# Moving zeros, source rows and half loads in the opening of a graph message-passing kernel on one Trainium2 core

## The chip, the core and the metric

The kernel runs on one core of one Trainium2 chip. The metric is the device time of one execution in microseconds (us). A core has five engines with their own instruction lists: PE (matrix products), DVE (vector), ACT (scalar functions), POOL (GpSimd, which also issues the indirect transfers) and SP (which issues nearly all other transfers). Sixteen DMA engines carry the transfers that SP and POOL issue.

## The reference

There are 6,250 nodes of 128 features and 200,000 edges, sorted by `dst`. Every edge has 20 attributes and a weight.

```python
def _L0_gnn_ref(atomic_embedding, pair_indices, f_ij, f_ij_cutoff, W_in, W_f1, b_f1, W_f2, b_f2, W_o1, b_o1, W_o2, b_o2):
    idx_i = pair_indices[0]
    idx_j = pair_indices[1]
    x = atomic_embedding @ W_in
    W_ij = shifted_softplus(f_ij @ W_f1 + b_f1) @ W_f2 + b_f2
    W_ij = W_ij * f_ij_cutoff
    x_ij = x[idx_j] * W_ij
    out = jax.ops.segment_sum(x_ij, idx_i, num_segments=N_ATOMS)
    return shifted_softplus(out @ W_o1 + b_o1) @ W_o2 + b_o2
edge_index = jnp.stack([src, dst])
h = jnp.maximum(_layernorm(x, axis=-1), 0.0)
x = x + _L0_gnn_ref(h, edge_index, edge_attr_20, edge_weight1, ...)
```

The gather goes by `dst`, which is sorted, and the sum by `src`, which is not.

## The kernel before, in words

**Quads and items.** The edges are cut into 391 quads of 512. The main loop at L1326 runs over items; item i holds the stages of several quads side by side. PE computes z of quad i+1 (`s1_pe`), ACT its softplus for quad i, DVE the one-hot rows `oh` of quad i (L379), PE the edge filter W (L561) and the gathered rows xg (L553) of quad i-1, DVE their product m (L576). Two quads are computed ahead of the loop. Steps that are not part of this pipeline hang on hooks: `at(i, point, fn, ...)` runs fn in item i at a named point. The point "L" stands first in an item and takes most loads; "D2" stands near its end. A hook's item thus sets its place in every engine's list, and SP issues strictly in that order. SP may have eight transfers under way: an issue waits for the eighth before it (the waits DMAHW0 to DMAHW7 in the order of instructions). POOL's are counted in the same way.

**Loads.** `load_sc(s)` (L337 to L357) loads what two quads need, a set: three parts of `ft`, the split edge attributes, from `fsd` (L344); two of `rb`, the relative node numbers, from `reld` (L348); and four windows `wn` of the node table `tab` (L355). Sets 0 and 1 are loaded ahead of the loop, set i/2 + 2 at the start of each even item. `fsd` is written by the kernel itself in blocks: `fb_load` (L312) brings a block of attributes, `fb_1` to `fb_4` split it in three, and L334 writes it. The largest value of a block is taken by `fb_max` (L321). `sb_load(k)` (L393) brings 16-bit source numbers, `sb`, for two quads to all partitions; it has four buffers.

**Where a sum goes.** From quad 8 on every second quad goes through a permutation on PE (pm, pt, pq, un). The others are compared with their own sources, either one by one (`eq`, L407; PE adds equal sources and copies them as s, L596) or, from quad 17, in pairs with a list (`eql`, L421; counted by PE as `lcnt`, L431). POOL then scatters their rows with an adding indirect transfer (L638) into one of four accumulators in memory. `acc_of(k)` picks the one for the k-th scatter: `K2_END` is where the turn among two, k % 2, becomes a turn among three, k % 3. A scatter that goes to the same accumulator as one before waits for that one to land.

**Zeros.** Each accumulator begins as zeros, written in ten pieces of 128 x 640 (320 KB, `zero_piece`, L201), and a few more for lists (`zero_list`, L205). POOL issues those of the first accumulator (three early, seven at L980) and of the second (L1011 to L1012), SP those of the third in the items of the list `Z2` and of the fourth in `Z3`. Between the first's zeros and the second's POOL copies one element, `gate` (L1010), out of the `wn` of set 1, and so waits until that has landed.

**The half pieces.** `base_i`, `reld` and the 16-bit sources `src16` are made from the raw numbers: for the first half of the kernel ahead of the loop, for the second half in two pieces. `half_load(k)` (L1043, L1044) brings a piece's `dst` and `src` numbers, two transfers of 196 KB. `half_piece(k)` has DVE compute `base_i`, `rel_f` and `rel_b` (L941 to L947), SP write `rel_b` to `reld` (L948), DVE narrow the sources (L891), SP write them to `src16` (L892), and DVE take the extent (`rel_ext`, L952, L953). `rel_b` lies in the one buffer named "x3" and the narrowed sources in the one buffer named "h". The same buffer "h" takes the output of the relu of the node table's next group (`prep_relu`, L271), which PE multiplies by W_in (L278).

Of the kernel before, what the change touches and what calls it, by code (L numbers as in the profile page):

```python
# [8 lines left out]
BF16 = mybir.dt.bfloat16  # L9
# [66 lines left out]
def tile_gnn(ctx: ExitStack, tc: tile.TileContext, x, fB, cT, srcT, srcr, srci, dstr, win_, wf1, wf2, bias, bo1c, wo1,  # L76
             wo2, consts, ident, cmap, out, n_edges):
    nc = tc.nc
# [9 lines left out]
    spread = big(NSC)  # L88
    NCH = -(-n_edges // P)
    NQ = -(-NCH // 4)  # L90
# [6 lines left out]
    GN = NP // GRP  # L97
    ZR = 10 if ACC_R % 10 == 0 else 1
    ZEARLY = 3
    K1_END, K2_END, K3_END = 0, 16, 170  # L100
    Z2, Z3 = [0, 1, 1, 2, 2, 3, 3, 4, 4, 5], range(18, 58, 4)
    mpq = sorted_quads(NQ)
    mpi = {q: n for n, q in enumerate(mpq)}
    rounds = unit_rounds(mpq)
# [92 lines left out]
    def zero_piece(eng, k, j, parts=1):  # L197
        v = accs[k][:ACC_R].rearrange("(p t) f -> p (t f)", p=P).rearrange("p (r e) -> r p e", r=ZR)
        w = ACC_R // ZR // parts
        for h in range(parts):  # L200
            eng.dma_start(v[j][:, h * w:(h + 1) * w], zero[:, :w])  # L201
# [692 lines left out]
    with tc.manual_schedule():  # L894
# [83 lines left out]
        nc.gpsimd.tensor_copy(b2rep, b2p.unsqueeze(1).to_broadcast([P, 4, P]))  # L978
        for j in range(ZEARLY, ZR):
            zero_piece(nc.gpsimd, 0, j)  # L980
        ms = []
        for i in range(2):
            m_ = cp.tile([P, 4, 132], F32, name=f"m{i}")
# [22 lines left out]
        sb_load(0)  # L1006
        if NQ > 2:
            load_sc(1)
            gate = cp.tile([1, 1], BF16, name="gate")
            nc.gpsimd.tensor_copy(gate, loads[1][2][0:1, 0, 0:1])  # L1010
        for j in range(ZR):  # L1011
            zero_piece(nc.gpsimd, 1, j)  # L1012
        if NB > 1:
            fb_load(1)
        hooks = {}
# [1 line left out]
        def at(i, point, fn, *a):  # L1017
            hooks.setdefault((i, point), []).append((fn, a))
# [8 lines left out]
            for fn, a in hooks.pop((i, point), []):  # L1027
                fn(*a)

        at(2 if spread else 0, "D2", rel_ext, 0, rel0)  # L1030
        if CE < EP // P:
            w = (CE + 4 * NS) // 2
            for i, a, b in ((8, CE, w), (10, w, 4 * NS), (13, CB, EP // P)):
# [17 lines left out]
            rel_ext(1 + k, r)  # L1051

        for k in range(2):
            at(k + 1 if spread else 0, "L", half_load, k)
            at(2 * k + 3 if spread else 0, "D2", half_piece, k)
        for j in range(ZR):
            at(Z2[j] if spread else 0, "L", zero_piece, nc.sync, 2, j)
        for j in range(ZR):
# [20 lines left out]
        for b in range(1, NB):  # L1079
            t0 = 2  # L1080
            if b > 1:
                t0 = 8 * b - 8
                while t0 + 1 not in mpi or t0 + 1 in units:
                    t0 -= 1
                at(max(0, t0 - 6), "L", fb_load, b)
            if b > 1:
                put("fmax", t0, fb_max, b)
            else:
                at(2, "D2", fb_max, b)
            put("f1", t0, fb_1, b)  # L1090
            put("f2", t0, fb_2, b)
            put("f3", t0, fb_3, b)
            put("f4", t0, fb_4, b)
# [118 lines left out]
        for r in range(-(-len(mpq) // RKQ)):  # L1212
# [10 lines left out]
            k = max(k + 1, i + AT["rk_slot"][0])  # L1223
            assert k <= i + 1
            at(k, AT["rk_slot"][1], rank_slot, r)
        for k in range(1, -(-NS // 2)):
            if not LB <= 2 * k < LE:
                at(max(0, splain[2 * k] - 4), "L", sb_load, k)
        for w in range(NW):
# [87 lines left out]
        for q in range(first):  # L1317
            s3_pe(q)
            s3_copy(q, 0)
            s3_copy(q, 1)  # L1320
            s3_idx(q)
            s3_ji(q)
            s3_scatter(q)
        consts_late()
        s1_pe(first)
        for i in range(max(NQ + 7, last + 22, r0_end + 2, lend + 24)):  # L1326
            if i % 2 == 0 and i // 2 + 2 <= (NQ - 1) // 2:
                load_sc(i // 2 + 2)
            run(i, "L")
            run(i, "D0")  # L1330
            if first <= i < NQ:
                s1_oh(i)
            run(i, "D1")
            if first <= i - 1 < NQ:
                s1_eq(i - 1)
            run(i, "PE0")
            if first <= i - 1 < NQ:
                s2_pe_x(i - 1)
            if first <= i and i + 1 < NQ:
                s1_pe(i + 1)  # L1340
            if first <= i - 1 < NQ:
                s2_pe_w(i - 1)
            run(i, "PEZ")
            if first <= i < NQ:
                s1_exp(i)
                run(i, "AE")
                s1_ln(i)
            else:
                run(i, "AE")
            if first <= i - 3 < NQ and not full[i - 1]:  # L1350
                s3_copy(i - 3, 0)
                s3_copy(i - 3, 1)
            run(i, "A0")
            if first <= i - 4 < NQ:
                s3_ji(i - 4)
            run(i, "A1")
            if first <= i - 1 < NQ:
                s2_copy(i - 1)
            run(i, "AX")
            run(i, "DM")  # L1360
            if first <= i - 1 < NQ:
                s2_m(i - 1)
            if first <= i - 3 < NQ:
                s3_idx(i - 3)
            run(i, "DR")
            run(i, "PE1")
            full[i] = sum(fn in banked for fn, _ in hooks.get((i, "PE2"), [])) > 2
            if first <= i - 2 < NQ:
                s3_pe(i - 2)
                if full[i]:  # L1370
                    s3_copy(i - 2, 0)
                    s3_copy(i - 2, 1)
            run(i, "PE2")
            run(i, "A2")
            run(i, "D2")
            if first <= i - 4 < NQ and plainq(i - 4):
                s3_scatter(i - 4)
            if first <= i - 2 < NQ and i - 2 not in mpi and not plainq(i - 2):
                s3_scatter(i - 2)
            run(i, "S")  # L1380
# [365 lines left out]
```

## Time and profile before

| | us |
|---|---|
| three timed runs | 1917.05, 1916.89, 1916.43 |
| their median | 1916.89 |
| the profiled execution's own time | 1913.6 |
| its span, first to last instruction | 1911.6 |

| engine | busy us | share of the span |
|---|---|---|
| PE | 1807.8 | 95% |
| DVE | 1656.5 | 87% |
| POOL | 1517.3 | 79% |
| ACT | 1476.1 | 77% |

The mean granted PE clock is 0.980 of full speed. The profile's times count from the start of the span. A timeline row has the start, the duration, the engine, the line of the code, the operation, what it writes and reads, and a count; in brackets stands the idle time of that engine just before, with what ended it. For SP (SPq) a row is the issue of a transfer, not its flight. Which wait ended last is inferred, so the name in brackets can be that of a semaphore that came last by the profile though another one held.

### The profile page before, as it was taken

The numbers are of one execution on the slowest core, as the hardware profiler recorded it, in microseconds if no ns is written. First come the engines' busy times: TensorE is split into PE (matmuls) and PEld (weight loads), VectorE is DVE, ScalarE is ACT, GpSimd is POOL, SyncE is SP. The second block draws the span as 40 slices with busy tenths as digits, with TensorE's granted clock in tenths as the row PEclk, the third lists the DMA queues.
The fourth block names the chain that finished last, engine by engine and source line by source line (L and its number), as shares of the span: only waits on it lengthen the run. The fifth ranks groups of instructions, "written<-read, shape, count | busy, mean of one in ns | idle before, by whom it ended". The sixth has DMA issues, their size and how long they took to land.

```text
span 1911.6 us, 58074 instructions
## 1 busy us (share of the span) xinstructions
PE 1807.8 (95%) x20601; PEld 1218.7 (64%) x20601; DVE 1656.5 (87%) x4692; ACT 1476.1 (77%) x4045; POOL 1517.3 (79%) x965
## 2 busy tenths in 40 slices
PE   4679999999999999999999999999999999999986
PEld 3556666666666666666666666666666666666654
DVE  5588998889999999999999889889889889888767
ACT  4579878878887878878887787787787787787725
POOL 4677887788886888888888888888888888878755
PEclk8799999999999999999999999999999999999998
DMA  8888787767775777776776677667666676666648
GB/s 286 205 175 167 155 179 140 132 120 131 139 134 114 131 129 128 132 148 119 128 138 127 123 128 129 117 130 127 116 129 129 115 130 126 118 116 134 106 100 268
DMA packets 351703, 267.55 MB, mean 140 GB/s; under 512 B 96719, under 2 KB 315258, under 8 KB 351410
## 3 DMA queue, kind: packets, MB, share of 16 engines
q1 hardware_dynamic: 218516, 197.30, 35.7%
q0 software_dynamic: 132336, 66.32, 34.7%
q8 instruction: 162, 2.65, 0.6%
q14 instruction: 131, 1.07, 0.2%
q10 hardware_dynamic: 558, 0.20, 0.0%
HBM read 154.65 MB, written 109.00 MB: 138 GB/s over the span
## 4 chain that ended last, share of the span: by engine, by line
PE 69%; DVE 16%; DMA 5%; POOL 2%; issue 2%; SPq 2%; ACT 1%; DVEq 0%; POOLq 0%; ACTq 0%
PE pq L743 20%; PE un L839 17%; PE W L561 13%; PE z L362 5%; PE po L756 4%; DVE pm L718 3%; PE xg L553 2%; PE W L550 2%; DMA acc<-s,lji 2%; DVE pt L732 2%; DVE so L824 2%; POOL acc L638 2%; DVE s L576 1%; DMA sb<-src 1%; DVE pt L576 1%
## 5 line engine op out<-in xcount | busy, mean ns | idle before, releaser
L638 POOL DMA_INDIRECT acc<-s,lji x751 | 1208.2, 1609 | 255.4 <-issue 176.2
L743 PE MATMUL pq<-pt,pm 128*128 128x387 bf16 x3056 | 582.9, 337 | 1.2 <-ACT s L596 0.6
L566 ACT ACTIVATE xc<-xg,cb 128x128 f32<-128x128 f32 x1564 | 448.0, 375 | 140.5 <-PE xg L553 130.6
L749 ACT CAST mst<-pq 128x387 bf16<-128x387 f32 x764 | 364.2, 487 | 93.0 <-PE pq L743 87.5
L561 PEld LDWEIGHTS W<-w,a 128*128 128x128 f32 x3128 | 421.6, 195 | 17.9 <-issue 6.9
L743 PEld LDWEIGHTS <-pm 128*128 128x128 bf16 x3056 | 294.3, 98 | 197.5 <-issue 4.5
L561 PE MATMUL W<-w,a 128*128 128x128 f32 x3128 | 419.9, 278 | 0.0
L839 PE MATMUL un<-so,mst 32*128 32x392 bf16 x9168 | 409.0, 325 | 9.4 <-DVE rank L685 4.3
L839 PEld LDWEIGHTS <-mst 32*128 32x128 bf16 x9168 | 240.4, 93 | 152.0 <-issue 16.7
L372 ACT ACTIVATE a<-a,con 128x512 f32<-128x512 f32 x391 | 282.5, 723 | 11.6
L732 DVE TENSOR_TENSOR pt<-pt 128x512 f32<-128x512 f32 x382 | 260.6, 682 | 0.0
L718 DVE TENSOR_SCALAR pm<-iotp,pos 128x576 bf16<-128x576 f16 x764 | 255.9, 395 | 0.0
L367 ACT ACTIVATE a<-z 128x512 f32<-128x512 f32 x391 | 236.4, 605 | 6.1 <-PE z L362 6.1
L850 DVE TENSOR_TENSOR accT<-un,accT 128x392 f32<-128x392 f32 x368 | 182.2, 556 | 47.8 <-PE un L839 47.4
L638 POOL DMA_INDIRECT acc<-os,oji x108 | 182.6, 1690 | 51.2 <-issue 12.2
L824 DVE TENSOR_SCALAR so<-iot,mst 128x392 bf16<-128x392 f16 x764 | 217.6, 335 | 2.1 <-PE un L839 2.0
L576 DVE TENSOR_TENSOR pt<-W,xc 128x512 f32<-128x512 f32 x191 | 131.5, 688 | 67.5 <-PE po L756 33.7
L362 PE MATMUL z<-ft,ws 123*128 123x512 bf16 x391 | 154.1, 395 | 17.2 <-DMA ft<-fsd 10.0
L576 DVE TENSOR_TENSOR s<-W,xc 128x512 f32<-128x512 f32 x188 | 128.5, 684 | 47.8 <-ACT xc L566 41.6
L553 PE MATMUL xg<-wn,oh 63*128 63x128 bf16 x1564 | 156.3, 221 | 13.2 <-DVE oh L379 11.3
L550 PE MATMUL W<-b2rep,onesb 64*128 64x512 bf16 x391 | 152.8, 391 | 0.0
L638 POOL DMA_INDIRECT acc<-s,ji x48 | 79.4, 1655 | 40.4 <-DMA acc<-s,ji 19.2
(216 smaller groups left out, 1794.2 us busy)
## 6 DMA issues: line engine op xcount, KB each, us to landing
rb<-reld SPq DMA_DIRECT2D x391, 64.0 KB
sb<-src SPq DMA_DIRECT2D x192, 128.0 KB
fsd<-f SPq DMA_DIRECT2D x49, 480.0 KB
ft<-fsd SPq DMA_DIRECT2D x195, 120.0 KB
fb<-in_fB_dram SPq DMA_DIRECT2D x49, 320.0 KB
ft<-fsd SPq DMA_DIRECT2D x195, 80.0 KB
wn<-tab SPq DMA_DIRECT2D x782, 15.8 KB
acc<-s,lji POOLq DMA_INDIRECT x751
```

Of the source, the lines that this page charges most:

```text
L362: nc.tensor.matmul(z, ws, ft[:K1, j * SEG:(j + 1) * SEG], start=True, stop=True)
L372: nc.scalar.activation(a, a, AF.Ln, bias=half, scale=0.5)
L561: nc.tensor.matmul(W[:, c, :], st[q]["a"][:, c * P:(c + 1) * P], w2, start=False, stop=(c == 3))
L566: nc.scalar.mul(xc[:, c, :], st[q]["xg"][:, c, :], late["c", q // CQ][:, 4 * (q % CQ) + c:4 * (q % CQ) + c + 1])
L576: nc.vector.tensor_tensor(m[:, :, :P], st[q]["W"], st[q]["xc"], op=ALU.mult)
L638: nc.gpsimd.indirect_dma_start(out=accs[k][:rows, :], out_offset=bass.IndirectOffsetOnAxis(ap=ji, axis=0), in_=s, in_offset=None, compute_ ...
L718: nc.vector.tensor_scalar(pm[:, c], iotp, rk[r]["pos"][:, 4 * j + c:4 * j + c + 1], None, op0=ALU.is_equal)
L732: nc.vector.tensor_tensor(pt[:, :, k * P:(k + 1) * P], a, high(a), op=ALU.subtract)
L743: nc.tensor.matmul(t[:, :PW], mp[q]["pm"][:, c, s * P:(s + 1) * P], high(mp[q]["pt"][:, c:c + 1, :PW])[:, 0], start=(c == 0), stop=(c == 3))
L749: nc.scalar.copy(mp[q]["ms", s][:, :PW], mp[q].pop(("q", s))[:, :PW])
L824: nc.vector.tensor_scalar(so, iotw[:, :GN], w[:, 3 * P // 2:3 * P // 2 + 1], None, op0=ALU.is_equal)
L839: nc.tensor.matmul(ts[g][:, :GN], mp[q]["ms", s][v, k * P:(k + 1) * P], mp[q]["oh"][v], start=(q == qs[0] and k == 0), stop=(q == qs[-1] a ...
```

## The change

The change edits no computation. It edits when steps of the opening are issued:

- `K2_END` goes from 16 to 24: eight more scatters take turns between two accumulators. `Z2` goes from items 0 to 5 to items 2 to 8.
- The second accumulator's ten zeros follow the first's seven on POOL directly; `gate` is gone.
- `sb_load(1)` is issued right behind set 1 and ahead of `fb_load(1)`, and no longer in the loop.
- `half_load(0)` and `(1)` go from items 1 and 2 to 4 and 5, `half_piece(0)` and `(1)` from items 3 and 5 to 6 and 7, `rel_ext(0)` from item 2 to 5, and `fb_max(1)` from item 2 to 3.
- z and `oh` of quad 2 stand ahead of `consts_late`, a row of small DVE steps.

```diff
-    K1_END, K2_END, K3_END = 0, 16, 170
-    Z2, Z3 = [0, 1, 1, 2, 2, 3, 3, 4, 4, 5], range(18, 58, 4)
+    K1_END, K2_END, K3_END = 0, 24, 170
+    Z2, Z3 = [2, 3, 4, 5, 5, 6, 6, 7, 7, 8], range(18, 58, 4)
...
         for j in range(ZEARLY, ZR):
             zero_piece(nc.gpsimd, 0, j)
+        for j in range(ZR):
+            zero_piece(nc.gpsimd, 1, j)
...
             load_sc(1)
-            gate = cp.tile([1, 1], BF16, name="gate")
-            nc.gpsimd.tensor_copy(gate, loads[1][2][0:1, 0, 0:1])
-        for j in range(ZR):
-            zero_piece(nc.gpsimd, 1, j)
+        if spread:
+            sb_load(1)
         if NB > 1:
             fb_load(1)
...
-        at(2 if spread else 0, "D2", rel_ext, 0, rel0)
+        at(5 if spread else 0, "D2", rel_ext, 0, rel0)
...
-            at(k + 1 if spread else 0, "L", half_load, k)
-            at(2 * k + 3 if spread else 0, "D2", half_piece, k)
+            at(k + 4 if spread else 0, "L", half_load, k)
+            at(k + 6 if spread else 0, "D2", half_piece, k)
...
-                at(2, "D2", fb_max, b)
+                at(3 if spread else 1, "D2", fb_max, b)
...
-        for k in range(1, -(-NS // 2)):
+        for k in range(2 if spread else 1, -(-NS // 2)):
...
-        consts_late()
         s1_pe(first)
+        s1_oh(first)
+        consts_late()
...
-            if first <= i < NQ:
+            if first < i < NQ:
                 s1_oh(i)
```

Three places show how the lists of SP and DVE read before and after. The first is SP's list between set 3 and set 4, before; `half` is a half load, `acc` from `zero` a zero piece, `xt` the node table's next group, `reld` and `src` the first half piece's two writes:

```order
L1043 DMA half<-in_dstr_dram 98x512 [waits DMAHW0_49]
L1044 DMA half<-in_srci_dram 98x512 [waits DMAHW1_49]
L201 DMA acc_77<-zero 128x640 [waits DMAHW2_49]
L201 DMA acc_77<-zero 128x640 [waits DMAHW3_49]
L393 DMA sb<-src_81 128x1024 [waits DMAHW4_49]
L201 DMA acc_77<-zero 128x640 [waits DMAHW5_49]
L201 DMA acc_77<-zero 128x640 [waits DMAHW6_49]
L225 DMA xt<-in_x_dram 128x256 [waits DMAHW7_49]
L948 DMA reld<-rel_b 98x512 [waits DMAHW0_49,DVE_49]
L892 DMA src_81<-s_523 98x512 [waits DMAHW1_49,DVE_49]
L334 DMA fsd<-f_468 128x3x640 [waits DMAHW2_49,DVE_49]
L344 DMA ft_120<-fsd 60x1024 [waits DMAHW3_49,DMAHW2_49,PE_49]
```

The same place in the changed kernel:

```order
L201 DMA acc_77<-zero 128x640 [waits DMAHW3_49]
L393 DMA sb<-src_81 128x1024 [waits DMAHW4_49]
L201 DMA acc_77<-zero 128x640 [waits DMAHW5_49]
L225 DMA xt<-in_x_dram 128x256 [waits DMAHW6_49]
L334 DMA fsd<-f_456 128x3x640 [waits DMAHW7_49,DVE_49]
L344 DMA ft_120<-fsd 60x1024 [waits DMAHW7_49,DMAHW0_49,PE_49]
```

Six issues stand less between set 3 and the write of `fsd`; ahead of set 3 a half load and three zeros have gone as well.

The second place is SP's list between set 5 and set 6 of the changed kernel (before, the writes of `reld` and `src` for the second half piece stood ahead of set 5, and those of the first ahead of set 4). It begins with the second of the two zeros behind set 5:

```order
L201 DMA acc_77<-zero 128x640 [waits DMAHW1_49]
L393 DMA sb<-src_81 128x512 [waits DMAHW2_49,DVE_49]
L393 DMA sb<-src_81 128x512 [waits DMAHW3_49]
L205 DMA acc_76<-zero 128x384 [waits DMAHW4_49]
L948 DMA reld<-rel_b 98x512 [waits DMAHW5_49]
L892 DMA src_81<-s_707 98x512 [waits DMAHW6_49]
L201 DMA acc_77<-zero 128x640 [waits DMAHW7_49]
L201 DMA acc_77<-zero 128x640 [waits DMAHW0_49]
L393 DMA sb<-src_81 128x512 [waits DMAHW1_49,DVE_49]
L393 DMA sb<-src_81 128x512 [waits DMAHW2_49]
L205 DMA acc_77<-zero 128x384 [waits DMAHW3_49]
L948 DMA reld<-rel_b 98x512 [waits DMAHW4_49]
```

Both pieces' writes now stand between set 5 and set 6, each behind source rows that wait for DVE, and the second's `src` write follows the last row.

The third place is DVE's list at the second half piece. Before, in item 5:

```order
L576 TENSOR_TENSOR m_255<-W,xc 128x4x128 [waits PE_49,Activation_49]
L612 SCALAR_TENSOR_TENSOR jf<-s,con,jd 128x4
L233 BN_STATS bn<-xt 128x6 [waits DMAHW7_49]
L233 BN_STATS bn<-xt 128x6
L235 BN_AGGR mv<-bn 128x2 [waits DVE_49] x2
L237 TENSOR_SCALAR var<-mv 128x2 [waits DVE_49]
L941 TENSOR_SCALAR base_i<-half,con 98x2 [waits DMAHW0_49]
L943 TENSOR_TENSOR rel_f<-half,base_i 98x512 [waits DVE_49]
L947 TENSOR_SCALAR rel_b<-rel_f 98x512 [waits DMAHW0_49,DVE_49]
L891 CAST s_651<-half 98x512 [waits DMAHW1_49]
```

The changed kernel, in item 7:

```order
L421 TENSOR_TENSOR eql<-sb,srcT_sb 128x1024 [waits DMAHW5_49,DMAHW4_49]
L576 TENSOR_TENSOR m_265<-W,xc 128x4x128 [waits PE_49,Activation_49]
L608 TENSOR_SCALAR jd<-srcT_sb,con 128x16
L612 SCALAR_TENSOR_TENSOR jf<-s,con,jd 128x4 [waits DVE_49]
L941 TENSOR_SCALAR base_i<-half,con 98x2 [waits DMAHW6_49]
L943 TENSOR_TENSOR rel_f<-half,base_i 98x512 [waits DVE_49]
L947 TENSOR_SCALAR rel_b<-rel_f 98x512 [waits DMAHW5_49,DVE_49]
L891 CAST s_795<-half 98x512 [waits DMAHW7_49,DMAHW6_49]
L952 TENSOR_REDUCE ext<-rel_f 98x1
L953 TENSOR_REDUCE ext<-rel_f 98x1
L325 TENSOR_TENSOR fr<-fb,f_766 128x640
```

The piece now stands behind the list's compare, and its `rel_b` and its narrowed sources wait for the transfers that free their one buffer each.

More of the change, by code (lines that the diff above doesn't have):

```diff
@@ L1323, in tile_gnn @@
             s3_scatter(q)
+        s1_pe(first)
+        s1_oh(first)
         consts_late()
-        s1_pe(first)
         for i in range(max(NQ + 7, last + 22, r0_end + 2, lend + 24)):
```

## The prediction, as put on record

> **What bounds the kernel now.** I read the table by stretch first. Its columns are the stretch in us, its length, and for each engine the busy us (with instructions), then the granted clock, the busy share of the DMA engines and GB/s.
>
> ```profile
> 25.00:30.00 5.00, 4.55 (x19) 3.56 (x19) 2.32 (x8) 2.42 (x7) 2.33 (x6) 1.00 0.63 194
> 30.00:35.00 5.00, 2.16 (x11) 1.88 (x12) 4.75 (x20) 3.87 (x9) 3.18 (x6) 0.73 1.03 406
> ...
> 80.00:90.00 10.00, 8.15 (x86) 7.32 (x86) 7.52 (x20) 9.28 (x28) 4.95 (x3) 0.82 0.63 155
> 90.00:100.00 10.00, 7.56 (x51) 5.34 (x50) 4.35 (x11) 7.20 (x20) 7.16 (x5) 0.83 0.87 213
> ...
> 150.00:200.00 50.00, 48.78 (x520) 32.66 (x519) 44.60 (x126) 44.58 (x126) 39.46 (x25) 1.00 0.81 171
> ```
>
> From 150 us on PE works 48.78 of 50 us: nothing moved in the opening can make that part shorter. The change acts in the opening, where PE has gaps, and its worth is how much earlier (or later) the kernel comes into the steady part. Second, I read the timelines of DVE, ACT and PE between 70 and 103 us for the idle times (start, us of work, instruction, and in brackets the idle time ahead and who ended it).
>
> ```profile
> 72.81 0.69 DVE L421 TENSOR_TENSOR eql<-sb,srcT_sb 128x1024 bf16<-128x1024 int16 x1 [4.41 <-DMA sb<-src]
> ...
> 78.00 0.38 ACT L271 ACTIVATE h<-hps 128x256 f32<-128x256 f32 x1 [10.60 <-DMA ft<-fsd]
> ...
> 84.51 0.69 DVE L421 TENSOR_TENSOR eql<-sb,srcT_sb 128x1024 bf16<-128x1024 int16 x1 [1.69 <-DMA sb<-src]
> ...
> 94.40 0.69 DVE L421 TENSOR_TENSOR eql<-sb,srcT_sb 128x1024 bf16<-128x1024 int16 x1 [3.40 <-DMA sb<-src]
> ...
> 97.94 0.82 DVE L321 TENSOR_REDUCE fmax<-fb 128x1 f32<-128x640 f32 x1 [2.25 <-DMA fb<-in_fB_dram]
> ...
> 101.60 0.69 DVE L421 TENSOR_TENSOR eql<-sb,srcT_sb 128x1024 bf16<-128x1024 int16 x1 [0.74 <-DMA sb<-src]
> ...
> 102.35 0.38 PE L431 MATMUL lcnt<-wgtb,eql 128*128 128x1 bf16 x8 [4.79 <-DVE eql L421]
> ```
>
> The waits are for loads that SP issues, so SP's place in its list decides. The relu at 78.00 is a case where the named releaser is not the true one. The relu writes buffer h, whose last content is the 16-bit copy of a half piece; it must wait until that copy's write, issued at 72.87 (row below), has landed: 5.1 us. I measure the change at two marks: that relu, and PE's lcnt at 102.35.
>
> **The change part by part.** SP's list from the third set of loads to the fifth is the first place. Columns as above; x1 to x4 are issues.
>
> ```profile
> 35.38 1.19 SPq L201 DMA_DIRECT2D acc<-zero  x1
> ...
> 39.28 1.07 SPq L1043 DMA_DIRECT2D half<-in_dstr_dram  x1
> 40.40 0.39 SPq L1044 DMA_DIRECT2D half<-in_srci_dram  x1
> 40.83 0.84 SPq L201 DMA_DIRECT2D acc<-zero  x2
> ...
> 52.39 2.40 SPq L201 DMA_DIRECT2D acc<-zero  x2
> 54.83 0.51 SPq L225 DMA_DIRECT2D xt<-in_x_dram  x1
> 55.44 1.56 SPq L948 DMA_DIRECT2D reld<-rel_b  x1
> ...
> 57.58 0.41 SPq L334 DMA_DIRECT2D fsd<-f  x1
> 61.88 1.09 SPq L344 DMA_DIRECT2D ft<-fsd  x3
> ...
> 65.21 1.76 SPq L355 DMA_DIRECT2D wn<-tab  x4
> ...
> 72.87 0.45 SPq L892 DMA_DIRECT2D src<-s  x1
> 74.54 1.11 SPq L344 DMA_DIRECT2D ft<-fsd  x3
> ...
> 78.25 1.76 SPq L355 DMA_DIRECT2D wn<-tab  x4
> 80.11 0.83 SPq L393 DMA_DIRECT2D sb<-src  x2
> ...
> 83.00 2.02 SPq L344 DMA_DIRECT2D ft<-fsd  x3
> ...
> 96.01 1.45 SPq L344 DMA_DIRECT2D ft<-fsd  x3
> ```
>
> *Ahead of the write of fsd (57.58), a gain.* Five of the third accumulator's zeros leave this stretch: 1.19 + 0.84 + 2.40 = 4.4 us. So do both half loads: 1.07 + 0.39 for the first and, at the bare 0.39 an issue, 0.8 for the second: 2.2 us. So do the first half piece's two writes: 1.56 + 0.45 = 2.0 us. Together 8.6 us. With no gate POOL's zeros start to fill the stretch 25 to 30, which ran at a DMA share of 0.63: up to 0.37 x 5 = 1.8 us of transfers come out of the crowd behind. The write of fsd would then go out at 57.6 - 8.6 - 1.8 = 47.2. Source rows for quads 2 and 3, now ahead of the second edge attributes, are on that same list and cost it nothing; they take away DVE's first long wait, below, and the front of DVE runs with this lead.
>
> *The lead is then paid back.* The half loads now stand behind the fourth set. From the write of fsd to its readers took 61.88 - 57.58 = 4.3 us, the set itself to 65.21 + 1.76 = 66.97, so 5.1 us: the first half load goes out at 47.2 + 4.3 + 5.1 = 56.6. DVE now stands at that half piece in item 6 without other work. Its rows of before, and the two waits behind transfers that give a landing:
>
> ```profile
> 43.90 0.76 DVE L407 TENSOR_TENSOR eq<-sb,srcT_sb 128x256 f32<-128x256 int16 x2 [6.05 <-DMA sb<-src]
> ...
> 59.51 0.49 DVE L233 BATCH_NORM_STATS2 bn<-xt 128x6 f32<-128x128 f32 x2 [4.50 <-DMA xt<-in_x_dram]
> ...
> 60.33 0.22 DVE L941 TENSOR_SCALAR base_i<-half,con 98x2 int32<-98x2 int32 x1
> ...
> 61.65 0.42 DVE L891 CAST s<-half 98x512 int16<-98x512 int32 x1
> ...
> 62.58 0.68 DVE L953 TENSOR_REDUCE ext<-rel_f 98x1 f32<-98x512 f32 x1
> ...
> 67.64 0.75 DVE L407 TENSOR_TENSOR eq<-sb,srcT_sb 128x256 f32<-128x256 int16 x2
> ...
> 74.42 0.83 DVE L325 TENSOR_TENSOR fr<-fb,f 128x640 f32<-128x640 f32 x1
> ...
> 75.46 0.74 DVE L407 TENSOR_TENSOR eq<-sb,srcT_sb 128x256 f32<-128x256 int16 x2
> ```
>
> A load landed in 59.51 - 54.83 = 4.7 us here. I take 4.7 for each landing, with bounds of 3.7 (a source row issued as the second of a pair at about 80.5 was used at 84.51: 4.0; one from 90.7 at 94.40: 3.7, by the same spacing) and 6.3 (a scatter, below). The half lands at 61.3; the piece takes 62.58 + 0.68 - 60.33 = 2.9, to 64.2. To the end of the compare at 67.64 + 0.75 DVE had 5.1 us of work, then the list compare of 0.69: 70.0 at the latest. SP meanwhile issues, from 56.6, four halves, three zeros, six source rows and a list's zeros: 14 at 0.83 / 2 = 0.42 each, 5.9, to 62.5. Then the fifth set, 78.25 + 1.76 - 74.54 = 5.5, to 68.0, and two zeros, to 68.8. Its next source rows wait for that list compare: 68.8 to 70.0, I take 69.4. Source rows 0.83, list zeros 0.45, then the first half's two writes, 0.45 each: the last goes out at 71.1.
>
> *A ring that before did not have.* Both half pieces now stand in succeeding items and share one buffer for each of their two results. The second piece's copy waits for the first piece's write: lands 71.1 + 4.7 = 75.8. From that copy to the end of the piece 62.58 + 0.68 - 61.65 = 1.6; then fr to the end of eq, 75.46 + 0.74 - 74.42 = 1.8: DVE is through at 79.2. Only that eq frees the buffer for SP's next source rows, behind which stand list, reld and the second half's write: 0.83 + 0.45 + 0.45, so the write goes out at 80.9 and lands at 85.6. The relu of item 8 waits for it: **85.6 against 78.00, 7.6 us later.** Had the halves' results two buffers each, all of this would hide.
>
> *The way back.* Behind the relu PE had 102.35 - 78.00 = 24.35 us to lcnt, of which DVE waited 1.69 + 3.40 + 2.25 + 0.74 = 8.1 us for loads. In the changed kernel those loads leave SP about when they did, while their reader is late: the waits go, 16.3 us remain, lcnt at 101.9 (-0.4). By PE's own work, 8.15 + 7.56 in the two stretches and about 1.7 at their ends, 17.4, it is 103.0 (+0.7). SP's own chain from 80.9 + 0.45, by the 96.01 - 83.00 = 13.0 us from the sixth set to the seventh, reaches the seventh at 94.4, 1.6 earlier than before. Between -1.6 and +0.7 I take **-0.5**: PE's side ends last, but not wholly.
>
> *Scatters.* These are GpSimd's rows.
>
> ```profile
> 81.23 1.54 POOL L638 DMA_INDIRECT acc<-s,ji  x1 [0.30 <-issue]
> 87.51 3.09 POOL L638 DMA_INDIRECT acc<-s,ji  x1 [4.74 <-DMA acc<-zero]
> ...
> 104.64 1.70 POOL L638 DMA_INDIRECT acc<-s,ji  x1 [0.30 <-issue]
> ```
>
> The wait at 87.51 is one that the new places of the zeros are about. I cost the scatters at nothing: the first buffer that a scatter has to free in the list phase is written here, with no wait on a scatter:
>
> ```profile
> 133.46 0.68 DVE L576 TENSOR_TENSOR s<-W,xc 128x512 f32<-128x512 f32 x1
> ```
>
> The eight scatters that now still alternate between two accumulators run behind the relu; if each waits for the last but one they come every 3.1 us (the longest row, 87.51), to 87.5 + 7 x 3.1 = 109.2 in place of 104.64, 4.6 us later. Between 109 and 133 lie 24 us, so nothing waits for them. If that cover failed, the 4.6 us would be paid.
>
> **A page that speaks against the change.** The rows: 30 to 35 ran at 406 GB/s and a share of 1.03 with POOL's zeros in flight. Ten ungated pieces of 327,680 bytes are 3.28 MB, 8.1 us at that rate, and now meet SP's second set. The Trainium skill (DMA: Bandwidth & Descriptors, "Queues, rings and completion order") says that each DMA engine goes round between the queues that have work, a packet at a time. No run so far shows the turns themselves; it is the third rival below.
>
> **Rivals.** *Faster: short landings.* The two halves of the ring and the half load land in 3.7 instead of 4.7 (3.0 us), the fsd step too in 3.7 instead of 4.3 (0.6), and SP's 1.2 us ahead of the fifth set (73.32 to 74.54) go: -0.5 - 4.8 = -5.3, 1911.6. For it: the 0.63 share in 80 to 90, so the transfers there have room. Against: the shares of 0.87 and 1.03 elsewhere. The Trainium skill (same page, "Anatomy of one DMA — SWDGE (gpsimd) path") fits 2.0 us plus bytes at 436 GB/s, an estimate of 2.2 us for a 100 KB write by that fit; the trace's 5.1 differs, and I go by the trace. Chance 0.31.
>
> *Slower: the ring stretches.* Each of its three landings takes what the scatter at 81.23 took until 87.51, 6.3 us: 3 x 1.6 = 4.8 more, -0.5 + 4.8 = +4.3, 1921.2. It decides once a landing is over 6.1 us (three times 1.4 more is +3.8). For it: those writes now leave among two zeros, two source rows and a list's zeros each. Against: the 5.1 us of before was among as many. Chance 0.13.
>
> *Slower: the ungated zeros take half the transfers from the second set.* Half of 8.1 us, 4.0, and the 1.8 us of filling not gained: -0.5 + 5.8 = +5.3, 1922.2. For it: the rate above. Against: 17 pieces were to move before 45 us anyhow. Chance 0.08.
>
> *Slower: two accumulators in turn throttle POOL* past the 24 us of cover: the eight would have to come at 6.3 us (87.51 - 81.23), 87.5 + 7 x 6.3 = 131.6, and the last of them land 6.3 later at 137.9, 4.4 us after 133.46: 1921.3. Chance 0.03.
>
> That the change does not do what it says, the first scatters starting no sooner since the zeros are as late, is inside the forecast, which gives them no worth.
>
> **How the numbers follow.** The profiled execution took 1913.6 us, 3.3 below the median of 1916.89; a difference carries over. 1916.9 - 0.5 = 1916.4. A measurement here can tell about 0.2%, 3.8 us, from no change, so the forecast is "same", chance 0.45; faster 0.31; slower 0.13 + 0.08 + 0.03 = 0.24. The range takes in the faster case with its end a little under 1911.6, 1910.5, and the ring's 1921.2, to 1921.5: what it leaves out is the third and fourth rival (0.11) and the tails of the first (some 0.09).
>
> **What would show it.** Right: fsd written near 47, DVE idle some 4 us ahead of the first half piece near 61, again ahead of the second half's copy near 76, the relu near 85.6, lcnt within a us or two of 102.35. Wrong: a relu below 81 (no ring, faster), or above 89 (slower); a write of fsd after 51 would mean that zeros held up the loads; a list product after 130 us that waits for a scatter would show the fourth rival.

## The result and the profile after

The changed kernel is slower: 1922.80 us against 1919.19 (medians of eight runs each), 1.0021 of the kernel before, with a 95% interval of 1.0011 to 1.0031, so 2 to 6 us, and about 4. A second measurement on another chip gave 1.0025 (1.0014 to 1.0036). The forecast was no change, 0.5 us less. It counted from 1916.89, the median of three runs. Over all eight runs the kernel before itself stands 2.3 us higher. So of the 6.4 us between 1922.8 and the forecast's 1916.4, 2.3 are the starting point, 0.5 the forecast gain and 3.6 the measured loss.

SP's timeline of the changed kernel, at the places that the prediction priced:

```profile
49.17 0.52 SPq L334 DMA_DIRECT2D fsd<-f  x1
57.10 1.11 SPq L344 DMA_DIRECT2D ft<-fsd  x3
...
60.44 1.77 SPq L355 DMA_DIRECT2D wn<-tab  x4
62.25 0.33 SPq L1043 DMA_DIRECT2D half<-in_dstr_dram  x1
...
67.11 3.47 SPq L393 DMA_DIRECT2D sb<-src  x4
70.68 0.38 SPq L205 DMA_DIRECT2D acc<-zero  x1
71.31 2.26 SPq L344 DMA_DIRECT2D ft<-fsd  x3
...
75.85 1.77 SPq L355 DMA_DIRECT2D wn<-tab  x4
...
80.41 0.47 SPq L948 DMA_DIRECT2D reld<-rel_b  x1
80.92 0.44 SPq L892 DMA_DIRECT2D src<-s  x1
81.41 1.45 SPq L201 DMA_DIRECT2D acc<-zero  x2
88.61 0.80 SPq L393 DMA_DIRECT2D sb<-src  x2
...
90.39 0.40 SPq L892 DMA_DIRECT2D src<-s  x1
```

The write of fsd does go out 8.4 us sooner than before. From then on the lead is spent: 22.1 us lie between it and set 5 (71.31), against 17.0 before. Then SP issues nothing for 5.8 us, from 82.86 to 88.61: it stands at source rows whose buffer DVE must free. DVE and ACT in the same stretch, and PE behind the relu:

```profile
65.32 0.23 DVE L941 TENSOR_SCALAR base_i<-half,con 98x2 int32<-98x2 int32 x1 [5.21 <-DMA half<-in_dstr_dram]
...
73.54 0.69 DVE L943 TENSOR_TENSOR rel_f<-half,base_i 98x512 f32<-98x512 int32 x1
84.96 0.43 DVE L947 TENSOR_SCALAR rel_b<-rel_f 98x512 bf16<-98x512 f32 x1 [10.73 <-DMA reld<-rel_b]
...
87.83 0.76 DVE L407 TENSOR_TENSOR eq<-sb,srcT_sb 128x256 f32<-128x256 int16 x2
```

```profile
93.56 0.38 ACT L271 ACTIVATE h<-hps 128x256 f32<-128x256 f32 x1 [30.97 <-DMA ft<-fsd]
```

```profile
93.99 1.23 PE L278 MATMUL xps<-win_sb,h 128*128 128x128 f32 x4 [21.09 <-ACT h L271]
```

This is the ring of the prediction, with one link in another place: the prediction had DVE wait at the second piece's copy for the first's `src` write, and in the trace it waits one step sooner, 10.73 us at `rel_b` for the first's `reld` write, since both `rel_b` need the same buffer. Only then comes the eq (to 88.59) that frees SP (88.61). SP's write of the second piece goes out at 90.39, and the relu, which needs its buffer, runs at 93.56. As in the kernel before, the name in the relu's bracket is not the true releaser; the same row of a second execution of the changed kernel (changed_again, below) has the write itself. PE waits 21.09 us.

```profile
94.02 0.38 ACT L271 ACTIVATE h<-hps 128x256 f32<-128x256 f32 x1 [29.94 <-DMA src<-s]
```

The table by stretch of the changed kernel shows what that does to the transfers (the seventh column of numbers is the clock, then DMA share and GB/s):

```profile
75.00:80.00 5.00, 0.00 (x0) 0.00 (x0) 0.00 (x0) 0.00 (x0) 3.73 (x3) 0.50 0.69 148
80.00:85.00 5.00, 0.00 (x0) 0.00 (x0) 0.04 (x1) 0.00 (x0) 0.00 (x0) 0.50 1.01 271
85.00:90.00 5.00, 0.00 (x0) 0.00 (x0) 4.33 (x11) 0.00 (x0) 0.00 (x0) 0.50 0.20 77
90.00:95.00 5.00, 1.01 (x4) 1.01 (x5) 0.00 (x0) 1.44 (x5) 0.00 (x0) 0.50 0.71 199
150.00:200.00 50.00, 48.78 (x522) 32.66 (x521) 42.51 (x122) 43.84 (x124) 38.92 (x25) 1.00 0.81 167
```

In the 15 us from 75 to 90 PE does nothing, and between 85 and 90 even the DMA engines are idle for four fifths of the time. The loss is made in the opening: from 150 to 200 us PE works 48.78 of 50 us in both kernels.

To follow all kernels with one ruler I take the start of ACT's exponential (L367), which runs once for each quad, from each timeline, and count its shift against the kernel before (31.98 us for quad 3, 81.49 for quad 9, 107.39 for quad 14, 137.03 for quad 20, quads counted from 0). Quad 9's waits for the relu, and from quad 20 on PE is nearly full. A second trace of the kernel before says what such a shift is worth. The kernels ran on several chips, on which the median of the kernel before lies between 1912.42 and 1919.19 us. Each ratio compares runs on one chip, while each shift counts from the one first trace of the kernel before, so a shift of less than 2 us tells little.

| kernel | time against before (95%) | relu, us | quad 3 | quad 9 | quad 14 | quad 20 |
|---|---|---|---|---|---|---|
| changed | 1.0021 (1.0011 to 1.0031) | 93.56 | +8.5 | +15.6 | +7.0 | +6.9 |
| changed_again | 1.0025 (1.0014 to 1.0036) | 94.02 | +9.7 | +16.0 | +9.1 | +7.1 |
| before_again | 1.0005 (0.9991 to 1.0019) | 77.56 | -0.5 | -0.4 | -0.2 | -1.8 |
| own_buffers | 1.0004 (0.9995 to 1.0012) | 69.79 | +7.9 | -4.0 | +3.4 | +1.7 |
| only_halves_late | 1.0028 (1.0018 to 1.0038) | 93.34 | +1.6 | +15.3 | +8.3 | +6.3 |
| halves_back | 1.0009 (1.0000 to 1.0018) | 75.13 | +9.0 | -2.9 | +1.0 | +2.2 |
| gate_kept | 1.0022 (1.0012 to 1.0031) | 90.80 | +2.1 | +12.8 | +5.7 | +4.2 |
| only_gate_gone | 1.0008 (0.9999 to 1.0016) | 79.92 | +6.3 | +1.9 | +2.2 | +1.3 |
| only_zeros_late | 0.9999 (0.9989 to 1.0008) | 74.82 | +0.2 | -3.2 | +1.4 | -0.1 |
| before_own_buffers | 0.9993 (0.9983 to 1.0004) | 70.77 | +1.2 | -3.5 | +1.6 | +1.2 |
| before_own_zeros | 0.9998 (0.9987 to 1.0008) | 65.88 | +0.3 | -9.0 | +1.3 | +1.6 |
| halves_back_own | 1.0005 (0.9996 to 1.0014) | 66.01 | +8.8 | -7.2 | +1.9 | +2.0 |
| zeros_in_halves | 1.0006 (0.9997 to 1.0014) | 81.50 | 0.0 | +3.5 | +4.6 | +4.0 |
| only_halves_150 | 1.0014 (1.0005 to 1.0023) | 66.99 | +0.4 | -8.2 | -4.6 | -4.7 |
| halves_item_150 | 1.0026 (1.0016 to 1.0036) | 66.48 | +9.7 | -8.5 | -0.3 | -0.3 |
| halves_and_zeros_out | 1.0042 (1.0027 to 1.0058) | 62.38 | +8.5 | -14.0 | -9.3 | -7.0 |
| zeros_later_30 | 1.0009 (0.9998 to 1.0019) | 63.57 | +0.6 | -10.8 | -4.1 | 0.0 |
| zeros_later | 1.0069 (1.0056 to 1.0082) | 62.87 | +1.0 | -10.5 | -3.0 | +11.5 |

### The profile page after: what moved, and what is told of

The parts are those of the page before. It is cut to its first block, busy times and chain, and to the rows that moved or that the text cites. A ratio compares the mean times of both kernels' runs of the same rounds, so it can differ in the third digit from the quotient of the medians.

```text
span 1920.9 us, 58069 instructions
## 1 busy us (share of the span) xinstructions
PE 1800.5 (94%) x20601; PEld 1219.8 (63%) x20601; DVE 1653.2 (86%) x4692; ACT 1472.4 (77%) x4045; POOL 1518.6 (79%) x964
## 5 line engine op out<-in xcount | busy, mean ns | idle before, releaser
L561 PEld LDWEIGHTS W<-w,a 128*128 128x128 f32 x3128 | 419.6, 195 | 16.3 <-issue 5.7
L839 PEld LDWEIGHTS <-mst 32*128 32x128 bf16 x9168 | 247.0, 93 | 147.4 <-issue 19.6
L367 ACT ACTIVATE a<-z 128x512 f32<-128x512 f32 x391 | 236.2, 604 | 6.7 <-PE z L362 6.7
L638 POOL DMA_INDIRECT acc<-os,oji x108 | 175.8, 1628 | 46.1 <-issue 15.9
L638 POOL DMA_INDIRECT acc<-s,ji x48 | 83.5, 1740 | 62.7 <-DMA acc<-s,ji 24.0
```

Of the source, the lines that this page charges most:

```text
L367: nc.scalar.activation(a, st[q]["z"], AF.Exp)
L561: nc.tensor.matmul(W[:, c, :], st[q]["a"][:, c * P:(c + 1) * P], w2, start=False, stop=(c == 3))
L638: nc.gpsimd.indirect_dma_start(out=accs[k][:rows, :], out_offset=bass.IndirectOffsetOnAxis(ap=ji, axis=0), in_=s, in_offset=None, compute_ ...
L839: nc.tensor.matmul(ts[g][:, :GN], mp[q]["ms", s][v, k * P:(k + 1) * P], mp[q]["oh"][v], start=(q == qs[0] and k == 0), stop=(q == qs[-1] a ...
```

## The experiments

My theory after the result was the ring; the rivals were the ungated zeros, the later zeros with the turn among two accumulators, and that nothing in the opening decides.

**own_buffers** takes the ring out of the changed kernel and nothing else:

```diff
-            r = rel(1, lo, hi, "x3", bufs=1)
-            src_cast(1, lo, hi, nc.vector, "h", bufs=1)
+            r = rel(1, lo, hi, "hrel", bufs=2)
+            src_cast(1, lo, hi, nc.vector, "hsrc", bufs=2)
```

> The changed kernel, with two buffers of their own for rel_b and for the narrowed sources of the half pieces, so that the second piece waits for no write of the first and the relu for none of the second. Ring theory: DVE's 10.73 us wait at rel_b of the second half piece and ACT's 30.97 us wait at the relu of item 8 go; the relu comes near 80 us in place of 93.56, quad 14's softplus (114.41 in the changed kernel, 107.39 before) near 106, and the time is 0 to 4 us under the kernel before. Rival, ungated zeros and long landings: the relu still comes after 88 and the time stays 3 to 5 us over before. Rival, two accumulators in turn: the relu comes early but the time stays over before.

The second piece runs without a wait and the relu comes 23.8 us sooner than in the changed kernel. DVE and then ACT of own_buffers:

```profile
73.14 0.69 DVE L943 TENSOR_TENSOR rel_f<-half,base_i 98x512 f32<-98x512 int32 x1
73.87 0.43 DVE L947 TENSOR_SCALAR rel_b<-rel_f 98x512 bf16<-98x512 f32 x1
```

```profile
69.79 0.39 ACT L271 ACTIVATE h<-hps 128x256 f32<-128x256 f32 x1 [7.87 <-PE hps L265]
```

The loss is gone, 1.0004 with 1 inside the interval. The buffers are all that changed, so the ring is the cause, and the rivals fall as the main cause of the loss. But no gain was left, and quad 14 was 3.4 us late where I expected it 1 us early, although the relu came 10 us sooner than I had expected.

**only_halves_late** puts the ring into the kernel before: the half loads and pieces move, all else stays.

```diff
-            at(k + 1 if spread else 0, "L", half_load, k)
-            at(2 * k + 3 if spread else 0, "D2", half_piece, k)
+            at(k + 4 if spread else 0, "L", half_load, k)
+            at(k + 6 if spread else 0, "D2", half_piece, k)
```

> The kernel before with one part of the change alone: half loads in items 4 and 5, half pieces in 6 and 7. Ring theory: the relu of item 8 comes 12 us or more later than 78.00, quad 14's softplus 4 to 8 us later than 107.39, time 3 to 8 us over before. Rivals: within 2 us of before.

```profile
83.86 0.43 DVE L947 TENSOR_SCALAR rel_b<-rel_f 98x512 bf16<-98x512 f32 x1 [8.53 <-DMA reld<-rel_b]
84.63 0.43 DVE L891 CAST s<-half 98x512 int16<-98x512 int32 x1 [0.35 <-DMA src<-s]
```

The same wait, the same late relu (93.34), and 1.0028. This one part of the change costs as much as the whole.

**halves_back** is the reverse: the changed kernel with those items (and `rel_ext(0)`, item 5 to 2) as before.

> The changed kernel with the half loads, half pieces and rel_ext(0) in their old items (1, 2; 3, 5; 2); the zeros, the early source rows and the turn among two up to 24 stay changed. Ring theory: no wait of DVE or ACT of over 8 us between 60 and 100, quad 14's softplus 1 to 5 us earlier than the 107.39 of before, time 1 to 5 us under before. Rivals (zeros, scatters): time 3 to 5 us over before, as in the changed kernel.

No wait of over 8 us is left on DVE. ACT, for which I had expected the same, keeps one of 10.11 us at the relu, as in the kernel before (10.60). I had also expected a gain and found none: 1.0009, its lower end at 1. The rest of the change is worth nothing, or costs up to 3.4 us (1.0018).

**gate_kept** and **only_gate_gone** price the ungated zeros. The first is the changed kernel with the gate back, as in the diff; the second is the kernel before with the same diff reversed.

```diff
-        for j in range(ZR):
-            zero_piece(nc.gpsimd, 1, j)
...
             load_sc(1)
+            gate = cp.tile([1, 1], BF16, name="gate")
+            nc.gpsimd.tensor_copy(gate, loads[1][2][0:1, 0, 0:1])
+        for j in range(ZR):
+            zero_piece(nc.gpsimd, 1, j)
```

> The changed kernel with the gate put back, so that the second accumulator's zeros wait for the second set's windows. Ring theory: the ring stays, the relu after 88 us, time 2 to 6 us over before. Rival, ungated zeros: set 1 and what follows it lands earlier, the write of fsd is read within 5 us, and the time comes to within 1 us of before or under it.

> The kernel before with only the gate gone, so that the second accumulator's ten zeros follow the first's on GpSimd at once. If these zeros take transfers from set 1 that the opening lacks: softplus of quads 3 to 5 4 to 9 us later than 31.98, 38.51, 40.76, as in the changed kernel, and quad 14 2 to 5 us later. If the bytes only change places: quads 3 to 5 late, quad 14 within 1.5 us, time within 1.5 us of before.

With the gate back the ring stays, the relu comes at 90.80, and the time is 1.0022, as expected. The two runs agree on what the gate does: without it quad 3 runs 6.3 us late in only_gate_gone, and with it back that delay falls from 8.5 to 2.1. In only_gate_gone the delay does not last: 1.3 us are left at quad 20, and the time is 1.0008 with 1 inside. So the zeros do delay what is loaded beside them. The third rival of the prediction had the direction right and the size wrong, since most of the lost time is got back behind them.

**only_zeros_late** is the kernel before with only the new `Z2` and `K2_END`.

> The kernel before with only the change's Z2 and K2_END. A part of the change that the other runs have not shown alone. Ring theory: no ring here, so within 2 us of before, quad 20 within 2.5 us of 137.03. Were the late zeros or the turn among two the costly part: 3 us or more over before.

It is level with the kernel before, in time and at quad 20. No part of the change but the late halves costs anything that these runs can tell. The early source rows, the later `fb_max` and the earlier z and `oh` of quad 2 were not run alone; they are in halves_back with the rest.

**Why nothing gains.** before_own_buffers gives the kernel before its own buffers, as in own_buffers; before_own_zeros adds the change's `Z2` and `K2_END`; halves_back_own adds the own buffers to halves_back.

> The kernel before with two buffers of their own for the half pieces' two results and nothing else. In before the relu of item 8 waits for the second piece's write, issued at 72.87, until 78.00. If what holds the opening is that chain: the relu at 74 or earlier, quad 20's softplus 2 to 5 us earlier than 137.03, time 1 to 5 us under before. If the loads behind it are as late as the relu: quad 20 within 1.5 us, time within 1.5 us of before.

> before_own_buffers with the change's Z2 and K2_END too (the gate, the source rows and the halves as before). The write of fsd goes out about 4 us sooner than in before_own_buffers as five zeros leave the list ahead of it; the zeros come back behind set 4. If the transfers of the whole opening bind: no better than before_own_buffers by over 1 us. If the list ahead of fsd binds: 2 us or more better.

> halves_back with the two buffers of their own. halves_back stood 2.2 us behind before at quad 20 though its relu was earlier (75.13); if the rest of its delay is in the loads behind the relu, this one stays within 1 us of halves_back; if it was the relu, 2 us or more earlier than it.

The relu of item 8 came at 70.77, 65.88 and 66.01 in place of 78.00, and the times are all within 0.1% of before. I had thought the relu's wait to be worth 2 to 5 us; it is worth none. before_own_zeros writes fsd 4.7 us sooner than before_own_buffers (53.27 and 58.02) and is no better for it. Its list compares show where the lead goes:

```profile
68.70 0.69 DVE L421 TENSOR_TENSOR eql<-sb,srcT_sb 128x1024 bf16<-128x1024 int16 x1 [3.52 <-DMA sb<-src]
...
83.55 0.69 DVE L421 TENSOR_TENSOR eql<-sb,srcT_sb 128x1024 bf16<-128x1024 int16 x1 [7.70 <-DMA sb<-src]
...
96.03 0.69 DVE L421 TENSOR_TENSOR eql<-sb,srcT_sb 128x1024 bf16<-128x1024 int16 x1 [5.58 <-DMA sb<-src]
...
110.33 0.69 DVE L421 TENSOR_TENSOR eql<-sb,srcT_sb 128x1024 bf16<-128x1024 int16 x1 [3.88 <-DMA sb<-src]
```

The four waits come to 20.7 us. In the kernel before the same four compares wait 4.41, 1.69 and 3.40 us (the prediction shows them) and, for the fourth,

```profile
108.46 0.76 DVE L421 TENSOR_TENSOR eql<-sb,srcT_sb 128x1024 bf16<-128x1024 int16 x1 [3.39 <-DMA sb<-src]
```

which is 12.9 us in all. What comes earlier waits here instead. My reading is that the loads of quads 9 to 14 stand behind all that SP has to move first, so that a change of order in that list changes where the waits are, not when the list ends. What takes work out of the list should then show, so three kernels take it out. **only_halves_150** and **halves_item_150** put the halves, first needed near quad 196, into items 148 to 159, of the kernel before and of the changed one. In both the half loads also get a buffer of their own. The diff is that of only_halves_150, without the line for this buffer:

```diff
-            at(k + 1 if spread else 0, "L", half_load, k)
-            at(2 * k + 3 if spread else 0, "D2", half_piece, k)
+            at(148 + 8 * k if spread else 0, "L", half_load, k)
+            at(151 + 8 * k if spread else 0, "D2", half_piece, k)
```

> The kernel before with the half loads and pieces moved to items 148 to 159 and nothing else. If transfers and SP's issues bound the opening: 2 to 5 us under before, the relu of item 8 near 73. If the place of the halves is free there: within 1.5 us of before.

> The changed kernel with the half loads in items 148 and 156, the pieces in 151 and 159, and a buffer of their own for the half loads; the half pieces are first needed near quad 196. Four loads of 196 KB and four writes of 98 KB, 1.2 MB, leave the opening: at about 300 GB/s, 4 us of transfers and eight issues on SP. If transfers bound the opening once the ring is gone: 2 to 5 us under own_buffers, so 1 to 4 us under before. If they don't: as own_buffers, within 1.5 us of before.

In the opening only_halves_150 does what was expected: 4.7 us ahead at quad 20, still 5.5 at quad 153. Then the two pieces take 8 us back, 4 each, and the kernel ends 1.0014. In its steady part DVE does the piece, and two items later PE waits for DVE:

```profile
736.77 0.21 DVE L941 TENSOR_SCALAR base_i<-half,con 98x2 int32<-98x2 int32 x1
...
739.01 0.68 DVE L953 TENSOR_REDUCE ext<-rel_f 98x1 f32<-98x512 f32 x1
```

```profile
745.30 0.89 PE L756 MATMUL po<-pt,pm 128*64 128x387 bf16 x8 [2.44 <-DVE accT L850]
...
786.07 0.89 PE L756 MATMUL po<-pt,pm 128*64 128x387 bf16 x8 [1.95 <-DVE accT L850]
```

The kernel before has no such wait there. The two account for 4.4 of the 8 us; the rest lies in shorter delays that I did not follow. The piece is 2.9 us of DVE in either place, and here nothing covers it. halves_item_150 shows the same loss, 9.0 us (-2.2 at quad 140, +6.8 at quad 180), from a nearly level start. In the opening its gain is smaller: at quad 20 it is 2.0 us ahead of own_buffers (-0.3 and +1.7). Taking the halves out takes away transfers, issues and DVE's work at once, and these runs do not say which of them the gain of 2 to 5 us is.

**halves_and_zeros_out** moves the third accumulator's zeros to items 8 to 17 as well, and so lets 40 scatters take turns between two accumulators.

```diff
-    K1_END, K2_END, K3_END = 0, 24, 170
-    Z2, Z3 = [2, 3, 4, 5, 5, 6, 6, 7, 7, 8], range(18, 58, 4)
+    K1_END, K2_END, K3_END = 0, 40, 170
+    Z2, Z3 = range(8, 18), range(18, 58, 4)
```

> halves_item_150 with the third accumulator's ten zeros in items 8 to 17 and the turn among two up to scatter 40: 3.3 MB more leave the stretch before 95 us, 11 us at 300 GB/s. Transfers as the bound: 3 to 8 us under before. Rival, two accumulators in turn: scatters come 2.5 to 3.1 us apart until the 40th, DVE waits for a scatter after 110 us, and the time is over that of halves_item_150.

Its quad 14 is 9.3 us ahead, the most of all. By quad 28 that is gone, +0.6:

```profile
146.80 0.69 DVE L576 TENSOR_TENSOR s<-W,xc 128x512 f32<-128x512 f32 x1 [4.58 <-DMA acc<-s,ji]
```

There DVE waits for a scatter, as my fourth rival had it, but with 40 in place of 24. The halves then cost their 8 us as above.

**zeros_in_halves** was to tell bytes from issues: the same ten zero pieces as twenty of half size.

```diff
-            at(Z2[j] if spread else 0, "L", zero_piece, nc.sync, 2, j)
+            at(Z2[j] if spread else 0, "L", zero_piece, nc.sync, 2, j, 2)
```

> The kernel before with the third accumulator's ten zero pieces as twenty of 160 KB: the same bytes, ten more issues on SP in the opening, 10 x 0.42 = 4.2 us of bare issue. If SP's issues bind the opening: quad 14's softplus 3 to 5 us later than 107.39, time 2 to 5 us over before. If the bytes bind: quad 14 within 2 us of 107.39 and time within 2 us of before.

Its trace has quad 20 4.0 us late, the bare price of ten issues; its time, 1.0006, allows 2.7 us at the most and none at the least. So bytes and issues stay unseparated: trace and time do not agree on the size.

**zeros_later** and **zeros_later_30** move only some zeros out, to items 4 to 12, from before_own_buffers (`K2_END` 26 and 30).

```diff
-    K1_END, K2_END, K3_END = 0, 16, 170
-    Z2, Z3 = [0, 1, 1, 2, 2, 3, 3, 4, 4, 5], range(18, 58, 4)
+    K1_END, K2_END, K3_END = 0, 30, 170
+    Z2, Z3 = [4, 5, 6, 7, 8, 9, 10, 11, 11, 12], range(18, 58, 4)
```

> before_own_buffers with the third accumulator's zeros in items 4 to 12 and the turn among two up to scatter 26: four of the ten pieces, 1.3 MB, leave the stretch up to about 95 us (4 us at 300 GB/s). If bytes bind the opening: quad 14 2 to 5 us earlier than in before_own_buffers (109.02), and with the turn among two only ten scatters longer the time is 1 to 4 us under before. If the zeros only collide with the later loads: within 1.5 us of before_own_buffers.

> zeros_later mended: the turn among two lasts to scatter 30, so that all ten zeros are issued ahead of the first scatter into the third accumulator and SP waits for none. Zeros in items 4 to 12, own buffers for the half pieces, all else as before. If bytes bind the opening: quad 14's softplus 2 to 5 us earlier than 107.39, no wait of over 8 us behind it, and the time 1 to 4 us under before. If the turn among two takes it back: quad 14 early, but quad 30 level with 177.25 or later, with a wait of DVE for a scatter.

With `K2_END` at 26 the last three zero pieces stand behind the first scatters into that accumulator, which they may wipe, and SP waits for those scatters:

```profile
103.02 0.34 SPq L306 DMA_DIRECT2D tab<-x  x1
115.17 0.80 SPq L201 DMA_DIRECT2D acc<-zero  x2
```

That is 11.8 us of idle SP, and all of its difference to the mended kernel; it says nothing on the theory. With 30, quad 14 is 4.1 us ahead, as expected, and quad 16 is level (-0.1). Its list compares again wait for source rows:

```profile
106.50 0.69 DVE L421 TENSOR_TENSOR eql<-sb,srcT_sb 128x1024 bf16<-128x1024 int16 x1 [5.06 <-DMA sb<-src]
111.47 0.69 DVE L421 TENSOR_TENSOR eql<-sb,srcT_sb 128x1024 bf16<-128x1024 int16 x1 [1.48 <-DMA sb<-src]
```

The zeros of items 10 to 12 lie among those loads: they were moved to the end of the opening, not out of it. No wait of DVE in this stretch is put down to a scatter, so the rival's sign did not come, though quad 30 is level as it said. The time is 1.0009, no gain, where I had expected one.

**changed_again** and **before_again** repeat the two kernels.

> The changed kernel once more, as it is, on the same chip as the others here. Ring theory: 3 to 6 us over before, quad 14's softplus 5 to 8 us later than 107.39, the relu of item 8 after 90. Were the 4 us of the first measurement an accident of that chip, it would lie within 1.5 us of before.

> The kernel before once more, for a second trace of it. The shifts of all traces are counted from one execution that lies under the median of its runs. If the opening repeats: quads 14 to 30 within 1.5 us of the first trace, so that a shift of 7 us at quad 20 is the change's, and what grows from there to the end is one execution's own. If the opening varies: some quad of these 3 us or more off, and the shifts count only against several traces.

The changed kernel's loss repeats. The opening of the kernel before repeats nearly as well: up to quad 12 its two traces differ by 0.6 us at most, behind it by up to 2.0 (quad 13), and at quads 18 to 21 by 1.5 to 1.8, a little over the 1.5 that I had allowed. From quad 20 to the last they part by 3 us more. The changed kernel is 7 us behind the one and 8.7 behind the other at quad 20, and the timed ratios allow 2 to 7. Both traces of the kernel before were executions faster than their medians, by 3 to 6 us (1913.6 and 1907.31, against 1916.89 and 1913.07). Why the timed loss is nearer to 4 than to 7 stays open.

## Why the prediction was wrong

*The ring that it named was right, and the sum was mis-sized ahead of it.* Forecast and measured, in us (the last column is what each step adds to the delay):

| mark | forecast | measured | added |
|---|---|---|---|
| write of fsd | 47.2 | 49.17 | +2.0 |
| set 4 begins (fsd has landed) | 51.5 | 57.10 | +3.6 |
| first half load | 56.6 | 62.25 | 0.0 |
| set 5 begins, 14 issues later | 62.5 | 71.31 | +3.2 |
| first piece's last write | 71.1 | 80.92 | +1.0 |
| second piece's write | 80.9 | 90.39 | -0.3 |
| relu of item 8 | 85.6 | 93.56 | -1.5 |

*The step that failed* is "the lead is then paid back": it took the durations of the kernel before (4.3 us from the write of fsd to its readers, 0.42 us an issue) for a list that had moved 8 us forward. In the changed kernel the landing took 7.9 us and the 14 issues 8.8 us, 3.47 of them for four source rows. With the two smaller terms of the table the relu was 8.0 us later than forecast.

SP did wait for fsd itself, as the view of its waits from 49 to 75 us says. But that long landing was not all crowding. The second line gives GB/s from 49 to 58 us in 40 equal slices of 0.225 us:

```profile
SPq L344 <- DMA fsd<-f: 7.3, 1, 7.3
```

```profile
GB/s 128 184 203 128 71 102 105 109 127 232 239 344 346 310 414 361 355 370 368 362 346 274 219 131 76 48 21 28 23 22 16 16 16 23 0 7 57 137 84 7
```

From 54.9 us on, until the readers go out at 57.10, the DMA engines move 28 GB/s or less: the end of fsd came late with the engines nearly idle. gate_kept (written at 47.51, read 7.83 us later) and own_buffers (48.55, 8.06) have the same long landing, so neither the ungated zeros nor the ring makes it. What does is open; in these runs a later write landed faster (before_own_zeros 53.27, 5.10; the kernel before 57.58, 4.30). The 14 issues were crowded: from 65 to 75 us the DMA share is 1.00 and more.

*A second term had the wrong sign.* The prediction took 1.8 us off for zeros that fill the stretch from 25 to 30. They did fill it, to a DMA share of 1.03, but fsd went out later for it: 49.17 without the gate and 47.51 with it (gate_kept), 59.11 in only_gate_gone and 57.58 in the kernel before. So having no gate cost about 1.6 us, where it was to gain 1.8 (the second traces, 50.37 of the changed kernel and 57.16 of the one before, make the cost larger). The first row shows only 2.0 of this, since the issues that left the list gained more than their 8.6 us: gate_kept writes fsd 10.1 us sooner than the kernel before.

*The ring* was seen, named and placed rightly but for the one link above, and its landings were if anything shorter than the 4.7 us taken: 3.1 us for the half (62.25 to 65.32), 4.6 for `reld` (80.41 to 84.96), 3.2 for `src` (90.39 to 93.56). So the rival that ended on the right side, "the ring stretches", had the right place and about the right time (1921.2 in place of 1922.8), but for a reason that did not come: landings of 6.3 us. Its sign of a relu after 89 came. That it was near is luck.

*The way back* was nearly right. The mark that it forecast at 101.9, the sixth group of eight lcnt products, begins at 110.95, inside this row, in which the fifth and sixth stand together:

```profile
110.75 0.54 PE L431 MATMUL lcnt<-wgtb,eql 128*128 128x1 bf16 x16
```

That is 17.4 us behind the relu, the figure that the prediction worked out from PE's own work, where its forecast took 16.3. So the sign "lcnt within a us or two of 102.35" failed by the delay of the relu, not by what came behind it: 8.0 us of late relu and a way back about as forecast give a kernel 7 us late at quad 20 in the trace.

*The faster rival* had its short landings, and they were of no use: the runs with an early relu and the same work in the opening (65.88, 66.01, 69.79, 70.77) all end level. *Scatters* cost nothing in the changed kernel, as forecast: only_zeros_late is level, and no wait of DVE or ACT between 93 and 260 us of the changed kernel is put down to a scatter. Two slips of the prediction's sums change nothing: three landings 1.4 us longer make +3.7, not +3.8, and the fourth rival's 4.4 us were added to 1916.9 and not to 1916.4.

## What to carry to other kernels

When a list of loads binds an opening, price a change by what it takes out of the list, not by what it moves forward in it: here moved work came back behind, and the durations read from the old order did not hold in the new one. Even the kernels that took work out of the opening did not end faster. What a new order can do is lose, where two steps that share one buffer come to stand next to each other and the second waits for the first's write; two buffers of 1 KB a partition for each of the two results took that loss away. And work that the opening can take may cost more elsewhere: two pieces of 2.9 us of DVE cost 4 us each in the steady part.

## What was not expected of the hardware

The last of a 480 KB write landed late while the DMA engines moved 28 GB/s or less, and the same write took 4.3 us to its readers in one order and 7.9 in another. Two executions differ, but not in one fixed place: the two traces of the kernel before agree within 0.6 us for 90 us and part by 3 us between quad 20 and the last, while the two of the changed kernel differ by up to 2.4 us in the opening (quad 13), by 0.2 at quad 20 and by 0.5 at the last quad. Cutting ten zero writes of 320 KB into twenty of 160 KB, the same bytes, put the trace 4 us back at quad 20, as much as ten bare issues, though the time moved by less.
